# A scheduled graph-network kernel: a priority table for each batch by itself, and batch 14's mirrored products taken back to TensorE

## The chip, the cores and the metric

The kernel runs on 1 core of one Trainium2 chip. Its time is the device time of one execution in microseconds (us); the figure for the kernel before is the median of 9 executions, 2457.01 us (2454.72 to 2459.84). Beside it there is a profile of one execution, from which all durations below are read. The engines are named as the profile names them: PE (TensorE, the matrix products; PEld is its loading of weights), DVE (VectorE), ACT (ScalarE), POOL (GpSimd) and SP (SyncE, which issues DMAs here and computes nothing).

## The reference

Sixteen batches of 1024 nodes with 128 features pass through four graph layers. Each layer first normalises and clips its input, and its result is added to `x`. All is float32.

```python
h = jnp.maximum(_layernorm(x, axis=-1), 0.0)          # ahead of each layer
# layer 0: three products in a row
h = h @ W + b
nh = h / jnp.maximum(jnp.linalg.norm(h, axis=-1, keepdims=True), EPS)
cos = jnp.einsum('bij,bkj->bik', nh, nh)              # 1024 x 1024, symmetric
h = jnp.einsum('bpq,bqc->bpc', edge_weight * cos, h)  # relu after the first two
# layer 1
x_agg = jnp.einsum('bnf,bnm->bmf', x, adjacency)
y = jnp.maximum(((1.0 + eps) * x + x_agg) @ W1 + b1, 0.0) @ W2 + b2
# layer 2
attn = jax.nn.softmax(where(att_mat > 0, tanh(s1[:, :, None] + s2[:, None, :]), NEG_INF), axis=-1)
last_h = jnp.einsum('bij,bjf->bif', attn, h)
# layer 3
e = jnp.einsum('bil,bkl->bik', h @ A, h)
e = e + jnp.swapaxes(e, 1, 2)                         # 1024 x 1024, symmetric
att = jax.nn.softmax(where(adj > 0, e, 0), axis=1) * adj
h_prime = relu(att @ h); i, f, o = three gates, each sigmoid(concat([x, h_prime]) @ w + b)
out = o * tanh(sigmoid(i * h_prime + f * x))
```

Each batch so has four symmetric 1024 x 1024 products: three in layer 0 (called products 0, 1 and 2 here) and one in layer 3 (product 3). Beside them stand the adjacency times features of layers 0 to 3, six accumulations over 1024 nodes.

## The kernel before, in words

A batch's nodes lie in 8 blocks of 128. A 1024 x 1024 matrix is made in 8 rows `j`, each in two halves `s` of 128 x 512 (one bank of PSUM). For a symmetric product only the blocks on and above the diagonal are multiplied (`sq`, line 768). The blocks below are mirrored from those above: the copies kept in the tile `above` are transposed on PE into the same bank (line 778), and what fills `above` is an ACT copy (line 800). For most batches the 4 x 4 quarter of blocks in the lower left goes another way (`Square`, `by_dma`): DVE transposes the right halves of rows 0 to 3 in squares of 32 x 32 into `above` (line 790), SP sends them to HBM in two parts (`by_hbm`, line 810), and eight DMAs bring them back with the squares in their places into the tile `got` (line 821), from which DVE reads the left halves of rows 4 to 7. The function `far` (line 533) says for which batches this holds: before, batches 1 to 14.

In a row, DVE turns the product into the weights of the accumulation: in layer 0 by `ew` (line 967); in layer 3 by `e` (line 1185, two halves), the row's largest value `top` (line 1197), an exponential on ACT (line 1201) that also gives the row's sum, its reciprocal (line 1215), a multiplication by the adjacency (line 1210) and a scaling of `hs` on ACT (line 1219). In batch 14 POOL does that multiplication for the odd rows (line 1206). Layer 2 has a tanh and an exponential per row on ACT (lines 1109, 1113) and one masking on DVE (line 1117). PE then adds the row to the accumulators (lines 830 and 841). Each layer starts with a normalisation on DVE, POOL (`rstd`, line 570) and ACT (lines 678 to 734), and layer 3 ends with gates (`finish`): in batch 14 its five wide steps stand on POOL (lines 1289, 1290, 1314), in batch 15 on DVE in two halves (lines 1296, 1308).

No order is written by hand. The kernel records every operation with an engine, an assumed duration, its reads and its writes. The class `Plan` then lists them (`order`): it keeps a clock for each engine, takes the engine whose next operation could start first, and among the operations of that engine that could start within `WINDOW` it issues the one with the smallest rank. The rank is a batch's deadline, less the length of the work that hangs on the operation, less a lead:

```python
lead = self.leads.get(o.key + o.edge, self.leads.get(o.key, 0.0))
o.rank = (self.deadline(o.batch) - o.tail - lead, o.seq)
```

A key is layer, engine and tile, such as `3 DVE e3`. The lead comes from the table `LEADS`: one value per key for all batches, with values of their own (`o.edge`) for batches 0, 1, 14 and 15. The deadlines are `PERIOD` 59 apart, batch 15's stands `LAST` 22 behind batch 14's. At most `AHEAD` 2 batches are open beyond the oldest. `POOLS` gives the number of buffers of each pool, and `KINDS` for each kind of tile the pool, the most buffers that it may hold and the most that batches younger than the oldest may hold. The listed order is what each engine's queue executes; an engine waits at an instruction whose inputs aren't there, and everything behind it in that queue waits too. Each batch's loads (`adjT`, `adjL`, `x`) and the round trips of `above` are issued in SP's queue, the stores of the result and the parameters in ACT's.

Of the kernel before, what the change touches and what calls it, by code (L numbers as in the profile page):

```python
# [53 lines left out]
class Plan:  # L54
# [53 lines left out]
    def link(self):  # L108
# [23 lines left out]
        for o in reversed(self.ops):  # L132
            o.tail = o.us + max((s.tail + o.lat for s in o.succs), default=0.0)
            lead = self.leads.get(o.key + o.edge, self.leads.get(o.key, 0.0))
            o.rank = (self.deadline(o.batch) - o.tail - lead, o.seq)
# [87 lines left out]
def tile_adj_preln(  # L223
# [67 lines left out]
    FLAGS = set("CabcdkxhyzTu")  # L291
# [34 lines left out]
    for load_it in first:  # L326
# [11 lines left out]
    POOLS = {"adjT": 16, "adjL": 5, "x": 3, "big": 13, "above": 2, "got": 1, "bank": 8, "small": 25, "row": 6, "hbm": 3, "hrow": 2}  # L338
    KINDS = {
        "adjT": ("adjT", 16, 16), "adjL": ("adjL", 5, 5), "x": ("x", 3, 3), "w4": ("big", 12, 12),  # L340
        "chunk": ("big", 9, 7), "above": ("above", 2, 1), "got": ("got", 1, 1), "ps": ("bank", 8, 7),
        "acc": ("bank", 7, 4), "small": ("small", 12, 8), "row": ("row", 5, 4), "hbm": ("hbm", 3, 2),
        "hrow": ("hrow", 2, 1),
    }
    PERIOD, LAST, AHEAD, WINDOW = 59.0, 22.0, 2, 0.05

    LEADS = {
        "0 ACT hT": -65.5, "0 DVE hn": -25.5, "0 DVE mv": 7, "0 DVE nb": -71, "0 DVE st": -1.5, "0 PE ps": -69,
        "0 POOL rstd": -10.5, "00 ACT above": 72.5, "00 ACT hT": -105.5, "00 ACT sq": 8, "00 DMA by": 83.5,
        "00 DMA got": 6.5, "00 DVE above": -17.5, "00 DVE ew": 50, "00 DVE h": -94, "00 DVE ss": -97,  # L350
        "00 PE acc0": -327, "00 PE ps": -234, "00 PE psP": 32, "00 PE sq": 124.5, "00 POOL rn": -50,
        "01 ACT above": 9, "01 ACT hT": 49, "01 ACT hTn": 145, "01 ACT sq": 358.5, "01 DMA by": -11.5,
        "01 DMA got": -20.5, "01 DVE above": 74.5, "01 DVE ew": 115, "01 DVE h": -7.5, "01 DVE ss": -16,
        "01 PE acc0": -170.5, "01 PE ps": -23, "01 PE sq": -68.5, "01 POOL rn": -16.5, "02 ACT above": -16,
        "02 ACT hTn": -101.5, "02 ACT sq": -56, "02 DMA by": -62, "02 DVE above": 3.5, "02 DVE ew": -96,
        "02 DVE ss": -6.5, "02 DVE x": -69, "02 PE acc0": -50.5, "02 PE ps": -19.5, "02 PE psP": 8.5,
        "02 PE sq": 284, "02 POOL rn": -16.5, "1 ACT g": 56.5, "1 ACT hn": 29, "1 ACT y1": 0.5,
        "1 DMA adjL": -175, "1 DVE adjL": 21, "1 DVE hn": -246.5, "1 DVE mv": 2, "1 DVE nb": -35.5,
        "1 DVE st": -772.5, "1 PE acc1": 3.5, "1 PE py": -151, "1 PE py2": -6.5, "1 POOL rstd": 31,
        "2 ACT e2": -115, "2 ACT h": 530.5, "2 ACT hfl": -66.5, "2 ACT hn": 7.5, "2 ACT hnT": 1.5,  # L360
        "2 ACT s1": -39.5, "2 DVE alone": -27.5, "2 DVE e2": 92, "2 DVE h": -0.5, "2 DVE hn": -12.5,
        "2 DVE hrow": -2.5, "2 DVE mv": 2.5, "2 DVE nb": 109, "2 DVE rden": -25.5, "2 DVE st": 10,
        "2 DVE x": 28.5, "2 PE acc2": 94.5, "2 PE p1": -12, "2 PE pf": -67.5, "2 PE ps": 9.5,
        "2 PE psP": -355.5, "2 POOL rstd": 5, "3 ACT above": -40, "3 ACT e3": 4, "3 ACT gT": -23.5,
        "3 ACT h3T": 51.5, "3 ACT hn": -43.5, "3 ACT hnT": 48.5, "3 ACT hp": 93.5, "3 ACT hpT": -21,
        "3 ACT z": -228, "3 DMA by": 11.5, "3 DMA z": -83.5, "3 DVE e3": -370, "3 DVE gate": 6.5,
        "3 DVE h": -79.5, "3 DVE hn": 217, "3 DVE mv": 16, "3 DVE nb": 220.5, "3 DVE st": -260.5,
        "3 DVE sum": -13, "3 DVE top": 42.5, "3 DVE z": -826, "3 PE acc3": -141.5, "3 PE pg": -19,
        "3 PE ps": 68.5, "3 PE psN": 171, "3 PE psP": 474.5, "3 POOL rstd": -22, "3 POOL z": -14,
        "T ACT adjT": 4, "T DMA adjT": -179, "T DVE adjT": -519.5, "x DMA x": -11.5, "0 ACT hT <0": -52.5,  # L370
        "0 ACT hT <1": 32, "0 ACT hT >0": -61, "0 ACT hT >1": 40.5, "0 ACT hn <0": -66, "0 ACT hn <1": -4.5,
        "0 ACT hn >0": 18.5, "0 ACT hn >1": -72, "0 DVE hn <0": -42.5, "0 DVE hn <1": 23.5,
        "0 DVE hn >0": -47.5, "0 DVE hn >1": -107, "0 DVE mv <0": 24, "0 DVE mv <1": 0, "0 DVE mv >0": 39,
        "0 DVE mv >1": 23, "0 DVE nb <0": -33.5, "0 DVE nb <1": -75, "0 DVE nb >0": 2, "0 DVE nb >1": -115.5,
        "0 DVE st <0": 3, "0 DVE st <1": 1, "0 DVE st >0": 23.5, "0 DVE st >1": -43, "0 PE ps <0": 63,
        "0 PE ps <1": -50.5, "0 PE ps >0": 49, "0 PE ps >1": 55.5, "0 POOL rstd <0": -5.5, "0 POOL rstd <1": 1,
        "0 POOL rstd >0": -83.5, "0 POOL rstd >1": -11, "00 ACT above <0": 25.5, "00 ACT above <1": 103.5,
        "00 ACT above >0": 141, "00 ACT above >1": 21, "00 ACT hT <0": -102.5, "00 ACT hT <1": -46,
        "00 ACT hT >0": 19.5, "00 ACT hT >1": 49, "00 ACT hTn <0": 0.5, "00 ACT hTn <1": 96.5,
        "00 ACT hTn >0": -73, "00 ACT hTn >1": -16.5, "00 ACT params <0": 1.5, "00 ACT sq <0": -4,  # L380
        "00 ACT sq <1": 120, "00 ACT sq >0": -83, "00 ACT sq >1": -5, "00 DMA by <1": -12, "00 DMA by >1": -1.5,
        "00 DMA got <1": 1.5, "00 DMA got >1": -3.5, "00 DMA params <0": -41.5, "00 DVE above <1": -252.5,
        "00 DVE above >1": -194, "00 DVE ew <0": 333, "00 DVE ew <1": 33.5, "00 DVE ew >0": -6.5,
        "00 DVE ew >1": -152, "00 DVE h <0": 0.5, "00 DVE h <1": 0.5, "00 DVE h >0": 4.5, "00 DVE h >1": 14,
        "00 DVE params <0": 391.5, "00 DVE ss <0": 4, "00 DVE ss <1": 8.5, "00 DVE ss >0": -1,
        "00 DVE ss >1": -7, "00 PE acc0 <0": -108, "00 PE acc0 <1": -172.5, "00 PE acc0 >0": -98,
        "00 PE acc0 >1": -312, "00 PE params <0": 79, "00 PE ps <0": 2.5, "00 PE ps <1": -117,
        "00 PE ps >0": -52.5, "00 PE ps >1": -107, "00 PE psP <0": 85, "00 PE psP <1": 42.5, "00 PE psP >0": 31,
        "00 PE psP >1": -14.5, "00 PE sq <0": 90, "00 PE sq <1": 185, "00 PE sq >0": 72, "00 PE sq >1": 250.5,
        "00 POOL rn <0": -42.5, "00 POOL rn <1": -48, "00 POOL rn >0": -46, "00 POOL rn >1": -25.5,  # L390
        "01 ACT above <0": 12.5, "01 ACT above <1": 11.5, "01 ACT above >0": -6.5, "01 ACT above >1": -1,
        "01 ACT hT <0": 52.5, "01 ACT hT <1": 93.5, "01 ACT hT >0": 38, "01 ACT hT >1": 24,
        "01 ACT hTn <0": 40.5, "01 ACT hTn <1": 110.5, "01 ACT hTn >0": 117.5, "01 ACT hTn >1": 107.5,
# [1049 lines left out]
```

## Time and profile before

| | |
|---|---|
| median of 9 executions | 2457.01 us (2454.72 to 2459.84) |
| the profiled execution: own time, span of its profile | 2459.84 us, 2458.0 us |
| PE busy | 2393.3 us, 97% of the span |
| DVE busy | 2118.3 us, 86% |
| ACT busy | 1270.8 us, 52% |
| POOL busy | 230.5 us, 9% |
| PE's share of the chain that ended last | 89% |
| moved by DMA | 271.75 MB, mean 111 GB/s |

A matmul in float32 leaves two records in the trace, a transpose on PE one. Their ends are modelled, and the records of one engine overlap; what a matmul costs PE in a dense stretch is the distance from its start to the next start. "Busy" merges such records, so that a short wait between two matmuls can be hidden under a record's end. PEclk is the clock that TensorE was granted, as a share of full speed.

### The profile page before, as it was taken

What the parts mean: (1) busy time and instruction counts of PE and PEld (TensorE: products, weight loads), DVE (VectorE), ACT (ScalarE), POOL (GpSimd) and SP (SyncE); (2) the same over time, 40 slices, a digit from 0 to 9 for tenths busy, and PEclk for the clock granted to TensorE, in tenths of its full rate; (3) what the DMA queues carried; (4) which work ended last, traced back from release to release, by engine and by line L of the source; (5) the groups of instructions that cost most, each with busy time, mean ns of one, the idle gap of its engine ahead of it and who ended that gap; (6) DMA issues with size and microseconds to landing.
All of it is one profiled execution on the core that took longest, in us unless ns stands there. A gap on an engine that the chain in (4) does not pass through costs nothing.

```text
span 2458.0 us, 34785 instructions
## 1 busy us (share of the span) xinstructions
PE 2393.3 (97%) x11882; PEld 1587.5 (65%) x11882; DVE 2118.3 (86%) x5280; ACT 1270.8 (52%) x2388; POOL 230.5 (9%) x141
## 2 busy tenths in 40 slices
PE   6999999999999999999999999999999999999995
PEld 3568576775757667576765766667576765665763
DVE  5758989899899989889898999989889899886586
ACT  3426564645545464463645545474464646543564
POOL 1001010100101001010101101001010110101012
PEclk9999999999999999999999999999999999999998
DMA  8831929658393774929657393874929568582010
GB/s 126 131 103 35 171 53 157 135 85 156 78 171 95 128 147 78 179 52 164 128 91 153 80 170 91 134 141 86 173 59 162 123 94 166 82 97 69 27 35 17
DMA packets 1171074, 271.75 MB, mean 111 GB/s; under 512 B 1005264, under 2 KB 1154512, under 8 KB 1170896
## 3 DMA queue, kind: packets, MB, share of 16 engines
q1 hardware_dynamic: 1149968, 260.12, 60.4%
q10 hardware_dynamic: 20928, 9.40, 1.4%
q8 instruction: 94, 1.54, 0.3%
q14 instruction: 84, 0.69, 0.1%
HBM read 202.33 MB, written 67.11 MB: 110 GB/s over the span
## 4 chain that ended last, share of the span: by engine, by line
PE 89%; DVE 4%; DMA 3%; ACT 2%; SPq 1%; issue 1%; POOL 0%; POOLq 0%; ACTq 0%; DVEq 0%
PE acc L830 34%; PE sq L768 18%; PE acc L841 17%; PE psP L608 5%; PE sq L778 4%; PE py L618 2%; PE py L1029 2%; PE ps_hTn L577 2%; PE pg L618 1%; PE ps_hnT L577 1%; PE psN L608 1%; DVE e L1185 1%; DMA by_hbm<-above 1%; DVE ew L967 1%; DMA got<-by_hbm 1%; PE ps_hT L577 1%
## 5 line engine op out<-in xcount | busy, mean ns | idle before, releaser
L830 PE MATMUL acc<-ew,h 128*128 128x512 f32 x1024 | 482.5, 597 | 6.6 <-DVE ew L967 6.5
L967 DVE SCALAR_TENSOR_TENSOR ew<-sq,rn,adjT 128x512 f32<-128x512 f32 x600 | 422.1, 738 | 36.7 <-PE sq L768 13.9
L768 PE MATMUL sq<-hTn 128*128 128x512 f32 (+3 forms) x1152 | 430.0, 488 | 0.4 <-ACT hTn L630 0.3
L800 ACT COPY above<-sq 128x256 f32<-128x256 f32 (+3 forms) x416 | 159.0, 386 | 471.2 <-PE sq L768 255.4
L768 PEld LDWEIGHTS sq<-hTn 128*128 128x128 f32 x1152 | 198.7, 191 | 147.1 <-issue 101.7
L830 PEld LDWEIGHTS acc<-ew,h 128*128 128x128 f32 x1024 | 180.0, 191 | 168.9 <-issue 130.1
L841 PEld LDWEIGHTS acc<-h,ew 128*128 128x128 f32 x2048 | 244.3, 192 | 31.8 <-issue 17.0
L830 PE MATMUL acc<-e,hs 128*128 128x512 f32 x512 | 247.3, 607 | 11.6 <-DVE e L1210 6.2
L841 PE MATMUL acc<-h,ew 128*128 128x128 f32 x2048 | 254.2, 275 | 0.1
L830 PE MATMUL acc<-adjL,hn 128*128 128x512 f32 x512 | 236.8, 598 | 4.8 <-ACT hn L734 4.8
L1201 ACT ACTIVATE e<-e,top 128x1024 f32<-128x1024 f32 x128 | 147.1, 1149 | 179.5 <-DVE top L1197 171.6
L841 PEld LDWEIGHTS acc<-h,e 128*128 128x128 f32 x2048 | 232.6, 192 | 11.1 <-issue 4.5
L841 PE MATMUL acc<-h,e 128*128 128x129 f32 x2048 | 234.3, 275 | 1.7 <-DVE e L1117 1.0
L570 POOL TENSOR_TENSOR rstd<-ve,mhalf 128x8 f32<-128x8 f32 x64 | 105.1, 1642 | 1250.2 <-DVE ve L689 1140.9
L898 ACT ACTIVATE adjT<-adjT 128x1024 f32<-128x1024 f32 x128 | 135.1, 1056 | 150.2 <-DVE adjT L895 104.0
L778 PEld LDWEIGHTS sq<-ident,above 128*128 128x128 f32 x896 | 118.9, 142 | 122.8 <-issue 92.4
L790 DVE STREAM_TRANSPOSE above<-sq 128x512 f32<-128x512 f32 x224 | 157.6, 707 | 35.1 <-PE sq L768 34.3
L895 DVE STREAM_TRANSPOSE adjT<-adjT 128x1024 f32<-128x1024 f32 x128 | 154.4, 1224 | 23.1 <-DMA adjT<-in_adj_dram 21.6
L778 PE MATMUL sq<-ident,above 128*128 128x128 f32 x896 | 165.9, 274 | 4.4 <-ACT above L800 4.4
L1117 DVE SCALAR_TENSOR_TENSOR e<-adjT,e 128x512 f32<-128x512 f32 x256 | 158.4, 679 | 7.5 <-ACT e L1113 7.4
L1210 DVE TENSOR_TENSOR e<-e,adjT 128x512 f32<-128x512 f32 x248 | 163.4, 679 | 0.0
L713 ACT ACTIVATE hn<-x,nb,rstd 128x128 f32<-128x128 f32 x256 | 105.4, 483 | 102.4 <-DVE nb L697 92.7
(130 smaller groups left out, 3507.2 us busy)
## 6 DMA issues: line engine op xcount, KB each, us to landing
adjT<-in_adj_dram SPq DMA_DIRECT2D x512, 128.0 KB, 4.3
adjL<-in_adj_dram SPq DMA_DIRECT2D x128, 512.0 KB, 5.0
by_hbm<-above SPq DMA_DIRECT2D x112, 512.0 KB, 4.2
got<-by_hbm SPq DMA_DIRECT2D x448, 128.0 KB, 3.9
x<-in_x_dram SPq DMA_DIRECT2D x15, 512.0 KB, 5.0
out_dram<-z ACTq DMA_DIRECT2D x15, 512.0 KB, 5.7
x<-in_x_dram SPq DMA_DIRECT2D x2, 256.0 KB, 4.6
out_dram<-z ACTq DMA_DIRECT2D x2, 256.0 KB, 2.7
```

What stands on the lines that cost most here:

```text
L608: nc.tensor.matmul(dst.t[:, (c - lo) * n : (c - lo + 1) * n], cols(srcT.t, c), w, start=True, stop=True)
L768: lambda: nc.tensor.matmul(dst.t[:, (first - lo) * P :], cols(leftT.t, j), span(rightT.t, first, hi), start=True, stop=True),
L778: nc.tensor.transpose(cols(dst.t, r), cols(above.t, p), ident)
L790: lambda: nc.vector.transpose(span(above.t, p, p + 4), read.t),
L800: lambda: nc.scalar.copy(span(above.t, p, p + hi - first), read.t[:, (first - lo) * P :]),
L830: lambda s=s, lo=lo, hi=hi: nc.tensor.matmul(acc[s].t, cols(h.t, at, w), span(ew.t, lo, hi), start=(j == 0), stop=(j == NB - 1)),
L841: nc.tensor.matmul(a.t[:, (c - lo) * n : (c - lo + 1) * n], cols(ew.t, c), h.t[:, at * w : at * w + n], start=(j == 0 and c == lo), stop=( ...
L895: dve(V(N), [t], [t], lambda t=t: nc.vector.transpose(t.t, t.t), True)
L967: lambda view=view, ew=ew, rn=rn, j=j, lo=lo, hi=hi: nc.vector.scalar_tensor_tensor(by_block(span(ew.t, lo, hi), D, 4), view(), rn.t[:, j ...
L1117: lambda e=e, j=j, lo=lo, hi=hi: nc.vector.scalar_tensor_tensor(span(e.t, lo, hi), span(aT[j].t, lo, hi), 0.0, span(e.t, lo, hi), op0=ALU. ...
L1201: lambda e=e, top=top, tot=tot: nc.scalar.activation(e.t[:, 0:N], e.t[:, 0:N], AF.Exp, bias=top.t, accum_out=tot.t),
L1210: lambda e=e, j=j, lo=lo, hi=hi: nc.vector.tensor_mul(span(e.t, lo, hi), span(e.t, lo, hi), span(aT[j].t, lo, hi)),
```

## The change

- The lead is looked up for each key and each batch: `LEADS[key]` is now a tuple of 16 values. The values are others throughout, and the special keys for the first and last two batches are gone. Where the old table's special values covered 4 of 16 batches, now the order of every batch may differ from its neighbour's.
- The flag `u` is gone, so that `far` holds for batches 1 to 13. Batch 14's four symmetric products mirror all their lower blocks on PE, as batches 0 and 15 do already: no round trip through HBM, and ACT copies where DVE transposed.
- `PERIOD` 59 becomes 60 and `LAST` 22 becomes 52: batch 15's deadline stands 52 behind batch 14's.
- `small` has 29 buffers in place of 25, and the shares in `KINDS` are others: `ps` may hold 5 of the 8 banks of PSUM (before 8, of which 7 for younger batches), `acc` 8 (before 7), `chunk` 11 (9), `w4` 12 of which 8 for younger batches (12), `small` 7 (12), `row` 3 (5).

```diff
-            lead = self.leads.get(o.key + o.edge, self.leads.get(o.key, 0.0))
+            lead = self.leads[o.key][o.batch] if o.key in self.leads else 0.0
...
-    FLAGS = set("CabcdkxhyzTu")
+    FLAGS = set("CabcdkxhyzT")
...
-    POOLS = {"adjT": 16, "adjL": 5, "x": 3, "big": 13, "above": 2, "got": 1, "bank": 8, "small": 25, "row": 6, "hbm": 3, "hrow": 2}
+    POOLS = {"adjT": 16, "adjL": 5, "x": 3, "big": 13, "above": 2, "got": 1, "bank": 8, "small": 29, "row": 6, "hbm": 3, "hrow": 2}
     KINDS = {
-        "adjT": ("adjT", 16, 16), "adjL": ("adjL", 5, 5), "x": ("x", 3, 3), "w4": ("big", 12, 12),
-        "chunk": ("big", 9, 7), "above": ("above", 2, 1), "got": ("got", 1, 1), "ps": ("bank", 8, 7),
-        "acc": ("bank", 7, 4), "small": ("small", 12, 8), "row": ("row", 5, 4), "hbm": ("hbm", 3, 2),
+        "adjT": ("adjT", 16, 16), "adjL": ("adjL", 5, 5), "x": ("x", 3, 3), "w4": ("big", 12, 8),
+        "chunk": ("big", 11, 4), "above": ("above", 2, 1), "got": ("got", 1, 1), "ps": ("bank", 5, 5),
+        "acc": ("bank", 8, 6), "small": ("small", 7, 6), "row": ("row", 3, 3), "hbm": ("hbm", 3, 2),
         "hrow": ("hrow", 2, 1),
     }
-    PERIOD, LAST, AHEAD, WINDOW = 59.0, 22.0, 2, 0.05
+    PERIOD, LAST, AHEAD, WINDOW = 60.0, 52.0, 2, 0.05
     LEADS = {
-        "0 ACT hT": -65.5, "0 DVE hn": -25.5, "0 DVE mv": 7, "0 DVE nb": -71, "0 DVE st": -1.5, "0 PE ps": -69,
...
-        "3 DVE e3": -370, "3 DVE e3 <0": -117.5, "3 DVE e3 <1": -399.5, "3 DVE e3 >0": -355, "3 DVE e3 >1": -521,
...
+        "3 DVE e3": (39.5, -336, -321, -314.5, -286.5, -296, -271, -307.5, -382, -319, -343.5, -253, -427, -402, -335, -152.5),
...
     }
...
-        o.edge = f" <{now[0]}" if now[0] < 2 else f" >{B - 1 - now[0]}" if now[0] > B - 3 else ""
```

(The five old values of `3 DVE e3` stand at different places of the old table and are brought together here.) The function that the flag reaches is unchanged:

```python
def far(b, product):
    return (b > 0 or "v" in FLAGS and product > 0) and b < (B - 1 if "u" in FLAGS else B - 2)
```

In the listed order of the changed program, against that of the program before, PE has 64 transposes more of line 778, DVE 16 transposes of 128 x 512 fewer (line 790), ACT 16 copies of 128 x 512 more (line 800), and SP 8 sends of line 810 and 32 loads of line 821 fewer. All other instructions are the same in number; most stand in another order from the first batch on.

## The prediction

> **What bounds the kernel now.** I read the page's busy shares, its forty slices, the busy time by stretches, the waits, and the timelines of PE and DVE at the end.
>
> ```profile
> PE 2393.3 (97%) x11882; PEld 1587.5 (65%) x11882; DVE 2118.3 (86%) x5280; ACT 1270.8 (52%) x2388; POOL 230.5 (9%) x141
> ...
> PE   6999999999999999999999999999999999999995
> ```
>
> ```profile
> 0.00:61.45 61.45, 38.62 (x148) 23.63 (x149) 36.33 (x100) 23.61 (x47) 8.92 (x11) 0.94 0.82 126
> ...
> 1045.00:1198.00 153.00, 153.00 (x775) 102.39 (x774) 139.66 (x356) 82.77 (x157) 13.33 (x8) 1.00 0.63 118
> ...
> 2397.00:2458.00 61.00, 34.99 (x115) 18.95 (x114) 37.04 (x82) 25.94 (x53) 14.87 (x7) 0.80 0.06 18
> ```
>
> In a stretch of the middle PE is busy for 153.00 of 153.00 us; only the first and the last slices have room. Busy time can hide short waits, so I price PE by distances from start to start:
>
> ```profile
> 1000.52 5.31 PE L830 MATMUL acc<-adjL,hn 128*128 128x512 f32 x12
> 1005.67 0.27 PE L778 MATMUL sq<-ident,above 128*128 128x128 f32 x1
> ...
> 2166.96 1.39 PE L830 MATMUL acc<-e,hs 128*128 128x512 f32 x2 [1.91 <-ACT e L1201]
> 2168.66 7.45 PE L830 MATMUL acc<-e,hs 128*128 128x512 f32 x14 [0.31 <-DVE e L1210]
> ...
> 2273.30 1.15 PE L778 MATMUL sq<-ident,above 128*128 128x128 f32 x9
> 2274.28 0.60 PE L577 MATMUL ps_hnT<-ident,hn 128*128 128x128 f32 x4
> ...
> 2276.37 12.67 PE L841 MATMUL acc<-h,ew 128*128 128x128 f32 x112
> 2288.88 1.95 PE L608 MATMUL psP<-w2e,hnT 128*128 128x130 f32 x16
> ...
> 2296.35 13.60 PE L830 MATMUL acc<-adjL,hn 128*128 128x512 f32 x26 [4.42 <-ACT hn L734]
> ...
> 2317.13 3.73 PE L1029 MATMUL py<-w,y 128*128 128x128 f32 x32
> 2320.70 6.86 PE L841 MATMUL acc<-h,e 128*128 128x129 f32 x60
> ...
> 2437.49 2.08 PE L608 MATMUL psN<-eye,hpT 128*128 128x131 f32 x16
> ```
>
> A record of 512 columns takes 5.15/12 = 0.429 us, a transpose 0.98/9 = 0.109, a record of 128 to 131 columns 12.51/112 = 0.112 (384 and 256 columns 0.322 and 0.215 in proportion). By the groups of shapes there are 3008, 1924, 6432, 256 and 256 of them: 1290 + 210 + 720 + 82 + 55 = about 2358 us of work at full rate. Some 100 of the span's 2458 us are left: 12 before the first matmul, 18 up to 61 us, 10 from there to 2089, 7 to 2289, 7 to 2321 (4.42 of it the wait at 2296.35), 45 from 2321 to the end, of which 18.6 lie behind PE's last matmul (2439.4). So nothing can be won in the middle; the change wins or loses in the last 170 us and by the work that it gives to PE.
>
> **The change, part by part.** The program's order, priced with these distances, has 2357.8 us of PE work before and 2364.8 after.
>
> *The flag.* 64 transposes more in batch 14: 64 x 0.109 = +7.0 us, on the path, since PE is full. DVE loses 16 transposes at 0.64 us from start to start, ACT gains 16 copies at 0.49, SP's queue loses 40 DMAs; ahead of 2289 us all of that lies beside PE, I cost it at nothing, and were PE's cover gone DVE's 10 us would be a gain. Behind 2289 it is in the walk below.
>
> *Deadlines, pools and shares* issue nothing; they act through the order alone.
>
> *The start.* SP's first 16 loads stand in the same order and the waits there end with `adjT` loads (DVE sits 5.01 and 5.36 us for them): 0, between -2 and +2.
>
> *The middle (61 to 2089).* All 13 batches are reordered. What I can read from the order is how much PE work stands between the last product of a row and its first accumulation, which is the time that DVE and ACT have. In layer 3 the least of a batch (2 to 11) was 9.1 us and is 10.0 to 12.1; in layer 0 the median of the rows was 2.5 to 3.8 and is 1.8 to 4.7. The round trip of `got` had at least 13 us of PE work in the three products of layer 0 and has 13 (42 and 40 in layer 3). Before, these distances sufficed without waits, so 0; the bounds are -5 (half of the 10 us that are there) and +18 (twelve batches with a wait of 1.5 us, the size of the wait at 2166.96).
>
> *2089 to 2289.* The wait at 2166.96 is batch 13's layer 3: there the least distance was 5.1 us, now it is 16.2. The wait and the half rate behind it (2 records in 1.70 us, 0.85 each) go: 7 us idle become 3, -4 (bounds 0 and -6).
>
> *2289 to 2321.* Batch 15's `x`, statistics, `rstd` and `hn` take 7.4 us behind the last `acc` of layer 0 (2288.9 to 2296.3). Before, 3.4 us of PE work stood there (line 608, 1072, 1098); now 8.1 us of batch 14's layer 2 do. Late next are the additions to the sixth and seventh `adjL` block, which stand on DVE behind batch 14's `hn`: I walk that to 2 us. 7 become 2.5: -4.5 (bounds 0 and -7).
>
> *From batch 15's last `py2` on.* Before, it ends at 2320.9, and 137.1 us follow with 92.5 us of PE work: layer 2 of both batches, then both layers 3 interleaved, batch 14's last. Now 80.1 us of work follow: batch 14's layer 3 runs beside batch 15's layer 2, then batch 15's layer 3 runs alone. I walk it with DVE's rows:
>
> ```profile
> 2392.63 1.29 DVE L1185 SCALAR_TENSOR_TENSOR e<-adjT,sq 128x512 f32<-128x512 f32 x2 [0.18 <-ACT above L800]
> 2393.95 1.22 DVE L1197 TENSOR_REDUCE top<-e 128x1 f32<-128x1024 f32 x1
> ...
> 2408.51 1.27 DVE L1210 TENSOR_TENSOR e<-e,adjT 128x512 f32<-128x512 f32 x2
> ```
>
> Start to start, a half row of line 1185, 1210 or 1117 costs 0.60, a `top` 1.13, a reciprocal 0.07. First the overlap: `py2` to `hrow` takes 11 us (before: 2320.9 to 2331.5). Then DVE has 14's rows and 15's maskings, 32.8 us, ACT 30 us of exponentials and copies beside it; I add 4 for DVE at exponentials and at POOL's four multiplications of 2.35. Layer 2's end and the next normalisation (lines 1130 to 1138, 652, 678, 687, 570, 706) take 9.5. Sum 57.3 with 48.5 of PE work: 9 idle. Then alone: from the transposes of `hn` to the first row 10 (11.5 for batch 14 at 2354.9, where `nb` came after `hn`); rows 16 x 0.60 + 8 x 1.13 + 8 x 0.07 + 16 x 0.60 = 28.8; 3 at their start, because batch 14's two `z` activations (2.2) stand ahead of the first exponentials on ACT; last accumulation, `hpT` and `psN` 5; the finish on DVE in halves 8.5, and the store 4.2 (2453.8 to 2458.0). Sum 59.5. Together 116.8 in place of 137.1: -20.3 (bounds -28, if DVE never waits and the prologue is 7; -10, if each of the two phases gets 5 us of waits more). `py2` itself ends 19.4 us of PE work later (2364.8 - 80.1 against 2357.8 - 92.5), the 7.0 among them.
>
> *The sum:* +19.4 - 4 - 4.5 - 20.3 = -9.4 us of the profiled span. That execution took 2459.84, 2.8 over the median; I take the difference over: 2457.0 - 9.4 = **2447.6 us**.
>
> [...] The row: a wait of 1.91 us already brought half rate (above), and in the last 61 us the granted clock is 0.80. So I took the prologue and the last accumulation at partly half rate. [...]
>
> **The rivals.**
> - *The overlap saves nothing.* The walk holds no waits that I did not look for. For it: before, ten waits of 0.5 to 2.9 us stand in the last 100 us. Against: they add up to some 13 us, and the walk is padded with 7. With 5 to 10 us more the time is 2452 to 2462, no change.
> - *The lone layer is paced by a cold PE.* Between its first row and its last, PE has 10.9 of products and 13.8 of accumulations, 24.7 us; at half rate 49, in place of DVE's 31.8: +17, 2465, slower. It decides from 29 us of half rate on, at a loss of half of it (14.3 us lead from -9.4 to +4.9). For it: the 0.80. Against: at full rate PE would be busy for three quarters of these rows.
> - *New waits in the middle.* With 1.5 us in each of twelve batches +18: 2466. For it: PE has no slack there, a wait is paid in full. Against: the distances above.
> - *Better still:* the unpadded walk, 2437 or less.
>
> The change can't do nothing: the order differs on each engine.
>
> **How the numbers follow.** No change is within 0.2%, 4.9 us, about what a measurement of this kernel can tell. Forecast (2437 to 2452) 0.63, better still 0.04, the saving eaten 0.17, cold PE 0.07, waits in the middle 0.09. Faster 0.67, same 0.17, slower 0.16. The range reaches from 2436 to 2462: 0.04 below, 0.16 above.
>
> **What would show it.** Right: line 778 with 960 records; PE busy 153 of 153 us in the middle; no wait of batch 13's layer 3 and none of 4 us at layer 1 of batch 15; about 13 us from the last matmul to the end in place of 18.6; 117 us from batch 15's last `py2` to the end. Wrong: waits of PE for `ew` or `e` spread over the middle, or a granted clock under 0.8 in the last 60 us.

## The result and the profile after

The changed kernel takes 2446.73 us, the median of 9 executions (2442.65 to 2450.59); the kernel before, run beside it, 2456.84 (29 executions, 2452.45 to 2461.88). The ratio is 0.9959, with a 95% interval of 0.9951 to 0.9967: 10.1 us less, or 0.41%. The prediction said 2447.6 and 9.4 us less. The profiled execution took 2447.29, its span is 2445.5.

The number was met, the reasons only in part. The page of the changed kernel, busy shares and PE's row of the forty slices, and below them the two lines of the chain of waits:

```profile
PE 2390.7 (98%) x11946; PEld 1587.3 (65%) x11946; DVE 2117.4 (87%) x5264; ACT 1283.2 (52%) x2404; POOL 232.0 (9%) x141
...
PE   6999999999999999999999999999999999999997
...
PE 81%; DVE 9%; DMA 5%; ACT 2%; SPq 2%; issue 1%; ACTq 0%; POOL 0%; DVEq 0%; POOLq 0%
PE acc L832 30%; PE acc L843 17%; PE sq L770 16%; PE psP L610 5%; PE sq L780 3%; DVE ew L969 3%; DMA got<-by_hbm 2%; DMA by_hbm<-above 2%; PE py L620 2%; PE py L1031 2%; PE ps_hTn L579 1%; PE pg L620 1%; DVE e L1187 1%; SPq L823 1%; DVE top L1199 1%
```

PE is busier (98% for 97%), and yet its share of the chain has fallen from 89% to 81%: DVE's `ew` and the round trip of `above` to `got` are on the path now. (Lines of the changed kernel stand two higher than those of before.) The stretches that answer to those shown of before, with time, busy us of each engine, granted clock of PE, DMA share and GB/s:

```profile
0.00:61.45 61.45, 41.09 (x161) 24.61 (x162) 38.15 (x105) 28.05 (x56) 8.92 (x11) 0.94 0.88 134
1045.00:1198.00 153.00, 152.88 (x762) 100.96 (x761) 141.48 (x357) 83.00 (x160) 13.32 (x8) 1.00 0.64 117
2384.50:2445.50 61.00, 43.61 (x167) 23.81 (x165) 43.54 (x113) 32.10 (x64) 11.86 (x6) 0.93 0.06 18
```

The stretch of the middle looks as full as before (152.88 for 153.00). That is a warning about a single stretch: the middle lost 14 us, in waits that stand elsewhere, and the same view of all of it, 61.45 to 2060 us, shows PE busy for 1985.45 us of 1998.55 where it was 1996.37. In the last 61 us PE is busy for 43.6 us in place of 35.0, at a clock of 0.93 in place of 0.80.

PE's timeline at the places of which the prediction spoke:

```profile
2307.43 8.21 PE L843 MATMUL acc<-h,e 128*128 128x129 f32 x72
2315.47 11.32 PE L832 MATMUL acc<-adjL,hn 128*128 128x512 f32 x26
...
2333.75 3.73 PE L1031 MATMUL py<-w,y 128*128 128x128 f32 x32
...
2422.45 10.55 PE L832 MATMUL acc<-e,hs 128*128 128x512 f32 x20 [1.92 <-DVE e L1212]
2432.84 2.05 PE L610 MATMUL psN<-eye,hpT 128*128 128x131 f32 x16
```

The first `acc` of batch 15's layer 1 (2315.47) has no wait before it any more, where 4.42 us stood; 8 us of batch 14's layer 2 lie in between (2307.43). Batch 15's last `py2` ends at 2337.3, and the program 108.2 us later, where it had been 137.3. From PE's last matmul to the end it is 10.8 us, where it had been 18.6. Line 780 (778 before) has 960 records, 64 more.

Priced as in the prediction (a stretch's length less its records times 0.429, 0.322, 0.215, 0.112 or 0.109 us), the time in which PE does no work at full rate is this. The third column starts where batch 14 begins to set the order; `py2` is batch 15's last.

| us | PE work | 0 to 61.45 | 61.45 to 2060 | 2060 to `py2` | behind `py2` | span |
|---|---|---|---|---|---|---|
| before | 2358.9 | 29.8 | 9.5 | 14.9 | 44.9 | 2458.0 |
| after | 2365.9 | 26.9 | 24.4 | 0.1 | 28.1 | 2445.5 |
| difference | +7.0 | -2.9 | +14.9 | -14.8 | -16.8 | -12.5 |

So the change gained 32 us in the last 385 us and 3 at the start, and gave back 7 for the transposes and 15 in the middle. (The two profiled executions differ by 12.5, the medians by 10.1: that of before was 2.8 above its median.)

The waits of PE in the middle, from 61 to 2060 us, in total, count and longest; before:

```profile
PE acc L830 <- DVE ew L967: 0.4, 2, 0.3
PE acc L830 <- ACT hn L734: 0.4, 1, 0.4
```

and after:

```profile
PE acc L832 <- DVE ew L969: 7.5, 10, 2.4
PE pf L1074 <- DVE hrow L1067: 3.0, 2, 1.6
```

Set against the program's order, nearly all of the `ew` waits are one place: the rows 4 to 7 of product 0, the first that read `got`, in batches 4 to 7 and 9 to 11. They hold 8.5 us of the time without work at full rate there (under 0.1 before). The two waits for `hrow` stand among the same rows of batches 12 and 13; with these two batches it is 12.0 us (0.5 before). Batch 9 has the longest wait. In SP's queue, DVE, POOL and PE of the changed kernel, around it:

```profile
1306.88 15.52 SPq L889 DMA_DIRECT2D adjT<-in_adj_dram  x16
1322.50 0.88 SPq L812 DMA_DIRECT2D by_hbm<-above  x1
...
1327.60 2.33 SPq L823 DMA_DIRECT2D got<-by_hbm  x4
```

```profile
1319.45 0.70 DVE L792 STREAM_TRANSPOSE above<-sq 128x512 f32<-128x512 f32 x1
...
1333.67 1.42 DVE L969 SCALAR_TENSOR_TENSOR ew<-got,rn,adjT 128x512 f32<-128x512 f32 x2 [1.41 <-DMA got<-by_hbm]
...
1335.09 3.06 DVE L969 SCALAR_TENSOR_TENSOR ew<-got,rn,adjT 128x512 f32<-128x512 f32 x2
...
1335.75 2.40 DVE L969 SCALAR_TENSOR_TENSOR ew<-got,rn,adjT 128x512 f32<-128x512 f32 x1
...
1338.07 0.74 DVE L969 SCALAR_TENSOR_TENSOR ew<-sq,rn,adjT 128x512 f32<-128x512 f32 x1
```

```profile
1335.32 2.28 POOL L1316 TENSOR_TENSOR z<-hn,gate 128x1024 f32<-128x1024 f32 x1 [4.38 <-DVE gate L1305]
```

```profile
1334.72 1.02 PE L832 MATMUL acc<-ew,h 128*128 128x512 f32 x2
1335.58 0.81 PE L770 MATMUL sq<-hTn 128*128 128x384 f32 x2
1336.22 0.27 PE L780 MATMUL sq<-ident,above 128*128 128x128 f32 x1
1338.86 1.13 PE L832 MATMUL acc<-ew,h 128*128 128x512 f32 x2 [2.37 <-DVE ew L969]
```

The squares are ready at 1320.15; their send waits in SP's queue behind 16 issues of `adjT` until 1322.50; the loads into `got` are issued at 1327.60, and DVE gets them at 1333.67, after 1.41 us of waiting. Then the four halves of rows 4 to 7 that read `got` come first in DVE's queue, and the right half of row 4 only at 1338.07. PE reaches the second accumulation of row 4 with 2.37 us to wait.

The row of 3.06 us holds two halves, and the second of them (the row of 1335.75) takes 2.40 us where such a half takes 0.74. It begins while POOL multiplies `hn` by a gate of an earlier batch into `z` (1335.32 to 1337.60), and it ends 0.55 us behind that product. Six halves of the changed kernel are held up in this way, in batches 6 and 8 to 12, for 2.13 to 2.40 us each; each ends 0.55 us behind POOL's product, and the 150 other halves of `ew` that read `got` take 0.75 at most. In batch 13 DVE's `alone` ahead of `hrow` is held up (1.50 us for 0.17). The four halves that read `sq` beside that product keep their 0.74 to 0.75. Before, the product was done 2 to 4 us ahead of the first of these halves in each of batches 4 to 13, and none of the 168 is held up; for the batch that is shown it ended at 1328.63 and the halves began at 1331.56:

```profile
1326.72 1.91 POOL L1314 TENSOR_TENSOR z<-hn,gate 128x1024 f32<-128x1024 f32 x1 [35.10 <-issue]
```

```profile
1331.56 2.74 DVE L967 SCALAR_TENSOR_TENSOR ew<-got,rn,adjT 128x512 f32<-128x512 f32 x4 [0.82 <-DMA got<-by_hbm]
```

So two things meet in the middle: `got` is late for the first accumulation of row 4 in batches 4, 5 and 7 (1.4 us of waits), and POOL's product holds DVE up in front of an accumulation of row 4 or of `hrow` in batches 6 and 9 to 13 (7.9 us of waits). If every held operation had taken its usual time, some 6.9 us of these 7.9 would not be there; that is an estimate from these rows, since no run here moved POOL's product alone.

The round trip itself is hardly longer than before. From the last transpose to DVE's first read of `got`, in batches 4 to 13, it takes 12.5 us on average (12.4 before). What differs is the order. Before, these batches have all the same one: 16.0 us of PE work from row 3's last product to the first accumulation of row 4, 19.1 to the second. After, each batch has its own: 14.2 to 17.6, and 18.2 to 19.1; and in batches 9 to 11 the small product `pf`, which waits for DVE's `hrow`, stands right behind that accumulation.

### The profile page after: what moved, and what is told of

Read it like the earlier page. It is cut to its first block, busy times and chain, and to the rows that moved or that the text cites. A ratio compares the mean times of both kernels' runs of the same rounds, so it can differ in the third digit from the quotient of the medians.

```text
span 2445.5 us, 34793 instructions
## 1 busy us (share of the span) xinstructions
PE 2390.7 (98%) x11946; PEld 1587.3 (65%) x11946; DVE 2117.4 (87%) x5264; ACT 1283.2 (52%) x2404; POOL 232.0 (9%) x141
## 3 DMA queue, kind: packets, MB, share of 16 engines
q8 instruction: 94, 1.54, 0.3%
## 4 chain that ended last, share of the span: by engine, by line
PE 81%; DVE 9%; DMA 5%; ACT 2%; SPq 2%; issue 1%; ACTq 0%; POOL 0%; DVEq 0%; POOLq 0%
PE acc L832 30%; PE acc L843 17%; PE sq L770 16%; PE psP L610 5%; PE sq L780 3%; DVE ew L969 3%; DMA got<-by_hbm 2%; DMA by_hbm<-above 2%; PE py L620 2%; PE py L1031 2%; PE ps_hTn L579 1%; PE pg L620 1%; DVE e L1187 1%; SPq L823 1%; DVE top L1199 1%
## 5 line engine op out<-in xcount | busy, mean ns | idle before, releaser
L832 PE MATMUL acc<-ew,h 128*128 128x512 f32 x1024 | 482.6, 596 | 13.5 <-DVE ew L969 13.4
L969 DVE SCALAR_TENSOR_TENSOR ew<-sq,rn,adjT 128x512 f32<-128x512 f32 x612 | 432.4, 738 | 57.8 <-ACT above L802 27.6
L802 ACT COPY above<-sq 128x256 f32<-128x256 f32 (+3 forms) x432 | 167.6, 394 | 399.1 <-PE sq L780 203.5
L843 PEld LDWEIGHTS acc<-h,e 128*128 128x128 f32 x2048 | 233.3, 192 | 14.9 <-issue 5.7
L780 PEld LDWEIGHTS sq<-ident,above 128*128 128x128 f32 x960 | 126.2, 142 | 123.6 <-issue 88.8
L780 PE MATMUL sq<-ident,above 128*128 128x128 f32 x960 | 175.2, 274 | 1.1 <-ACT above L802 0.8
L792 DVE STREAM_TRANSPOSE above<-sq 128x512 f32<-128x512 f32 x208 | 146.5, 707 | 21.3 <-PE sq L770 20.4
```

The costliest lines, as they stand in the source:

```text
L780: nc.tensor.transpose(cols(dst.t, r), cols(above.t, p), ident)
L792: lambda: nc.vector.transpose(span(above.t, p, p + 4), read.t),
L802: lambda: nc.scalar.copy(span(above.t, p, p + hi - first), read.t[:, (first - lo) * P :]),
L832: lambda s=s, lo=lo, hi=hi: nc.tensor.matmul(acc[s].t, cols(h.t, at, w), span(ew.t, lo, hi), start=(j == 0), stop=(j == NB - 1)),
L843: nc.tensor.matmul(a.t[:, (c - lo) * n : (c - lo + 1) * n], cols(ew.t, c), h.t[:, at * w : at * w + n], start=(j == 0 and c == lo), stop=( ...
L969: lambda view=view, ew=ew, rn=rn, j=j, lo=lo, hi=hi: nc.vector.scalar_tensor_tensor(by_block(span(ew.t, lo, hi), D, 4), view(), rn.t[:, j ...
```

## The experiments

In e2, e3, e5, e6 and e9 the planner ranks by two tables or deadlines, one up to a switch and the other from there on, with the shares that belong to each; so the middle of one kernel is joined to the end of the other. Their line numbers are up to 148 higher. The flag `u` is out in all of the kernels below, so their operations are those of the changed kernel, but for what e4, e7, e8 and e9 add or move. The "lone layer" is batch 15's layer 3, which stands alone behind all other work.

| | median, us | ratio to before, 95% interval |
|---|---|---|
| changed kernel | 2446.73 | 0.9959 [0.9951, 0.9967] |
| e1 flag alone | 2459.15 | 1.0005 [0.9996, 1.0013] |
| e2 changed middle, old end | 2467.50 | 1.0038 [1.0024, 1.0052] |
| e3 old middle, changed end | 2434.59 | 0.9906 [0.9892, 0.9920] |
| e4 send from ACT's queue | 2458.94 | 1.0005 [0.9996, 1.0013] |
| e5 = e3 with the old deadline | 2452.41 | 0.9978 [0.9968, 0.9988] |
| e6 = e1 with the new deadline at the end | 2453.19 | 0.9980 [0.9969, 0.9991] |
| e7 `top` twice in the lone layer | 2457.42 | 0.9998 [0.9989, 1.0007] |
| e8 transposes twice in the lone layer | 2446.78 | 0.9952 [0.9939, 0.9964] |
| e9 = e3 with three rows on POOL | 2431.90 | 0.9900 [0.9885, 0.9915] |
| e10 right half of row 4 first | 2444.73 | 0.9949 [0.9937, 0.9962] |

And where PE did no work at full rate, from one profile of each:

| us | 0 to 61.45 | 61.45 to 2060 | 2060 to `py2` | behind `py2` | `py2` to the end |
|---|---|---|---|---|---|
| e1 | 29.0 | 11.3 | 10.9 | 40.8 | 139.2 |
| e2 | 27.7 | 24.3 | 10.0 | 39.1 | 137.6 |
| e3 | 30.3 | 8.3 | 0.3 | 28.2 | 108.2 |
| e4 | 26.9 | 34.9 | 0.1 | 27.9 | 108.1 |
| e5 | 29.4 | 9.2 | 1.0 | 46.4 | 128.7 |
| e6 | 29.0 | 10.9 | 21.1 | 27.7 | 121.9 |
| e7 | 26.9 | 23.2 | 0.1 | 37.8 | 118.0 |
| e8 | 27.7 | 22.5 | 0.1 | 24.9 | 108.1 |
| e9 | 29.4 | 8.3 | 0.2 | 25.8 | 105.8 |
| e10 | 28.1 | 21.2 | -0.1 | 28.2 | 108.2 |

### e1: the flag alone

```diff
-    FLAGS = set("CabcdkxhyzTu")
+    FLAGS = set("CabcdkxhyzT")
```

> The kernel before with nothing changed but the flag u, so that batch 14 mirrors its quarter on PE: 64 transposes more, 16 transposes of DVE fewer, 40 DMAs fewer, the old table, old deadlines and shares. By the prediction's step the 64 transposes of 0.109 us are paid in full: 2456.8 + 7.0 = 2463.8, ratio 1.0028. The rival: DVE loses 16 x 0.64 = 10 us in batch 14, and the last 140 us of the old order are set by DVE; then part or all of the 7 comes back there, and the time is between 2455 and 2459.

The work of PE grows by the 7.0 us, but the time by 1.2 (0.05%, between -1.0 and +3.2): the rival holds. Beside the profile of before, 4.0 us come back between 2060 and `py2` and 4.1 behind it, where DVE's 16 transposes and the round trips of batch 14 are gone. So with the old table the 64 transposes are nearly free; the new table with the flag was not run.

### e2 and e3: the two middles and the two ends exchanged

In both the planner got

```diff
             o.rank = (self.deadline(o.batch) - o.tail - lead, o.seq)
+            early = self.early[o.key][o.batch] if o.key in self.early else 0.0
+            o.rank_early = (min(o.batch * self.due[0], (self.batches - 2) * self.due[0] + self.due[1]) - o.tail - early, o.seq)
...
-                        pool, most, share = self.kinds[k]
+                        pool, most, share = (self.early_kinds if oldest < self.switch else self.kinds)[k]
...
-                key=lambda f: f[1].rank,
+                key=lambda f: f[1].rank_early if oldest < self.switch else f[1].rank,
```

with the changed table early and `switch` 13 in e2, the old table early and `switch` 12 in e3.

> Spliced in the planner: as long as the oldest open batch is below 13 the operations are ranked with the changed table, deadlines and shares, from there on with the old ones; the flag u is out, so the operations are those of the changed kernel. It is to be read against the run with the flag alone, which has the same operations and the same end of the order. If the 24 us in which PE doesn't work between 61 and 2089 us of the changed kernel (10 before) belong to its order, this run is 8 to 14 us slower than the flag alone. If they are an accident of the one profiled execution, it is within 2 us of the flag alone.

> The splice the other way round: old table, deadlines and shares while the oldest open batch is below 12, the changed ones from there on; flag u out. If the changed kernel wins in its last 350 us and loses in the middle, this one has both good parts: idle in the middle 10 to 12 us in place of 24, from batch 15's last py2 to the end 108 us as in the changed kernel, time 2432 to 2438, ratio about 0.991. If the good end depends on how the batches stand when it begins, or if the waits of the middle come with batch 14 on PE and not with the table, the time is 2444 or more, as in the changed kernel.

e2 is 8.3 us slower than e1, which has the same operations and the same end. Its middle is idle for 24.3 us as in the changed kernel, and the same waits are there, with six `got` halves held up by POOL's product again (1.70 to 2.40 us). PE's waits from 61 to 2060 us in e2:

```profile
PE acc L978 <- DVE ew L1115: 6.6, 10, 2.5
PE pf L1220 <- DVE hrow L1213: 1.6, 2, 0.8
```

and in e3, the longest that there is, beside a second of the same length:

```profile
PE sq L924 <- ACT above L946: 0.3, 1, 0.3
```

e3 takes 2434.59 us, 24.6 less than e1 and 12.1 less than the changed kernel; its end is that of the changed kernel to a tenth (28.2 idle, 108.2 us from `py2` on). In e3 no half that reads `got` takes over 0.77 us. So the waits of the middle belong to the new table and shares (the two were not parted) and not to one execution, nor to batch 14's flag, and the good end doesn't depend on that middle. The two parts of the change can be had apart, and their sum is near: e1 + 8.3 - 24.6 = 2442.9, against 2446.73.

### e4: the second send of product 0 from ACT's queue

```diff
-                lambda: nc.sync.dma_start(
+                lambda: (nc.scalar if lo == 2 and self.k.endswith("_0") else nc.sync).dma_start(
```

> The changed kernel; only the second send of product 0 (by_hbm, rows 2 and 3) is issued from ACT's queue in place of SP's, where in batches 4 to 12 it stands behind the 16 to 32 issues of the adjT loads and goes out 0.3 to 3 us after its data is there. If SP's queue makes the first row that reads got late, the waits of PE for ew_4 of product 0 (7.6 us in batches 4 to 11) shrink to 2 or less and the time goes to 2439 to 2442. If the flight of the DMAs itself sets the round trip, the waits and the time stay (2446 +- 1.5). If ACT is held up by the issue and the wait in its queue, new waits of PE for ACT appear and it is slower than the changed kernel.

It is 12.2 us slower than the changed kernel, as the third case had it, but not for the reason given there: PE's waits for ACT in the middle grew by 0.6 us only (1.3 to 1.9). The send went out hardly earlier, because in ACT's queue it stands behind other work: on average over batches 4 to 13 it left 1.25 us after the last transpose, in place of 1.54. And the rest of the round trip grew, so that DVE got `got` 13.5 us after the last transpose in place of 12.5. The middle has 10.5 us more of idle PE, of which 7.6 stand at rows 4 to 7 of product 0. The trip grew in six of the ten batches (4, 5, 6, 10, 12 and 13, by 0.9 to 3.2 us) and shrank in the other four (by 0.2 to 0.8), and the idle time at these rows grew in the same six and shrank in the same four. The experiment failed as a cure for SP's queue, and why the later part of the trip grew was not settled. That an earlier send would win was not shown. What the ten batches do show is that in this order a longer round trip is paid where it falls.

### e5 and e6: deadline and leads of the end

e5 is e3 with

```diff
-    PERIOD, LAST, AHEAD, WINDOW = 60.0, 52.0, 2, 0.05
+    PERIOD, LAST, AHEAD, WINDOW = 59.0, 22.0, 2, 0.05
```

and e6 is e1 with `switch` 12, behind which the old table and the old shares go on with 60.0 and 52.0.

> As the run with the old middle and the changed end (2434.6 us), but the deadlines of the end are the old ones too: batch 15's stands 22 behind batch 14's in place of 52. Table and shares of the end stay the changed ones. If the end is won because batch 15's layer 3 comes alone, behind batch 14's, and the deadline brings that, both layers 3 are interleaved again, the idle time of PE behind batch 15's last py2 goes back from 28 us to 41 to 45, and the time is 2447 to 2452. If the leads of batches 14 and 15 carry the end by themselves, it stays at 2434 to 2438.

> As the run with the flag alone (2459.2 us: old table, old shares, flag u out), but from the time at which batch 12 is the oldest on batch 15's deadline stands 52 behind batch 14's and PERIOD is 60. If the deadline is the cause of the shorter end, the part behind batch 15's last py2, less the PE work in it, goes from 41 us to 28, and the time to 2445 to 2449. If it needs the new leads as well, the idle time ahead of py2 (11 us there) grows by what is won behind it or the end keeps its 41 us, and the time is 2456 or more.

e5: without the new deadline the end is lost, 46.4 us of idle in place of 28.2, and 17.8 us of time. PE's waits there:

```profile
2331.98 2.10 PE L723 MATMUL ps_hnT<-ident,hn 128*128 128x128 f32 x8 [7.64 <-DVE hn L852]
...
2380.21 2.08 PE L976 MATMUL acc<-e,hs 128*128 128x512 f32 x2 [6.71 <-DVE e L1356]
```

e6: the deadline alone brings the short end (27.7 us idle), but ahead of it the idle time grows from 10.9 to 21.1, and the time falls by 6.0 us only. (Its profiled execution was 3.2 us over its median.) The accumulations of the two layers 3 show the same: in e5 batch 15's begin at 2407.4, ahead of the end of batch 14's (2418.7); in e6 they follow each other (2415.0 and 2415.9), as they do in the changed kernel, with more room (2389.6 and 2410.7). The wait ahead of batch 15's layer 1, which the changed kernel has lost, is there as in the kernel before:

```profile
2307.64 4.63 PE L978 MATMUL acc<-adjL,hn 128*128 128x512 f32 x5 [4.42 <-ACT hn L882]
```

Neither theory holds by itself. The deadline is what shortens the part behind `py2`; the new leads, with the new shares that come with them, are what keeps the part ahead of it free of waits (21.1 to 0.3 us, e6 against e3).

### e7 and e8: what paces batch 15's lone layer

```diff
-                lambda e=e, top=top: nc.vector.tensor_reduce(top.t, e.t[:, 0:N], axis=AX.X, op=ALU.max, negate=True),
+                lambda e=e, top=top: [
+                    nc.vector.tensor_reduce(top.t, e.t[:, 0:N], axis=AX.X, op=ALU.max, negate=True)
+                    for _ in range(2 if b == B - 1 else 1)
+                ],
```

```diff
-                    for r, p in enumerate(at):
-                        nc.tensor.transpose(cols(dst.t, r), cols(above.t, p), ident)
+                    for r, p in enumerate(at * (2 if self.k == "15_3" else 1)):
+                        nc.tensor.transpose(cols(dst.t, r % len(at)), cols(above.t, p), ident)
```

> The changed kernel; in batch 15's layer 3 each row's top is computed twice (8 reductions of 1.13 us more on DVE, the second writes the same values, the listed order is the same). If DVE paces that lone layer, the time grows by 8 to 10 us, to 2455 to 2457. If PE paces it (24.7 us of matmuls and transposes between first row and last, in 29.8 us), DVE has room and it grows by 4 or less.

> The changed kernel; in batch 15's layer 3 each mirrored block is transposed twice on PE (112 transposes of 0.109 us more, 12.2 us, the second writes the same values). If DVE paces the lone layer the time grows by 0 to 5 us (the added work lies in PE's waits), if PE does, by 10 to 12.

The 8 reductions of 1.13 us, 9.0 us, lengthen the part behind `py2` by 9.8 us and the time by 10.7: they are paid in full. The expectation of e8 has a wrong count: 112 blocks are mirrored in the four products of a batch, in the one product of layer 3 it is 28, so 3.06 us were added and not 12.2. They cost nothing that can be seen (+0.05 us in the medians, with intervals of some 3 us either way; the end is 108.1 us long, its idle time 3.2 less). DVE paces the lone layer. One stretch of the changed kernel's profile says the same, from the first `e` to the last:

```profile
2400.44:2430.20 29.76, 23.57 (x75) 11.56 (x74) 29.41 (x48) 18.26 (x35) 6.60 (x4) 0.94 0.06 18
```

DVE (the third busy time) works for 29.41 of 29.76 us, PE for 23.57.

### e9: three rows on POOL

e3 with

```diff
-            if ("5" in FLAGS or "z" in FLAGS and (b == B - 2 if "T" in FLAGS else b >= B - 2)) and j % 2:
+            if (b == B - 2 and j % 2 or b == B - 1 and j in (0, 1, 3)):
```

(and the condition of the loop below it changed in the same way).

> As the run with the old middle and the changed end (2434.6 us), but in batch 15's layer 3 POOL multiplies rows 0, 1 and 3 by the adjacency, as it does for the odd rows of batch 14: DVE loses 6 halves of 0.60 us, 3.6 us. If DVE paces the lone layer, the time falls by 2 to 3.6, to 2431 to 2432.5. If a multiplication of 2.35 us on POOL takes longer than the row has, the accumulations wait for it and the time stays at 2434.6 or grows.

2431.90 us, 2.7 less than e3 by the medians (by the ratios 1.5, and their intervals overlap); the end is 2.4 us shorter, of the 3.6 that DVE is spared. That is about the same price from the other side, and the fastest kernel here: 0.9900 of before, 14.8 us under the changed kernel.

### e10: the right half of row 4 first

The changed kernel with its listed order changed by hand in product 0 of batches 4 to 11:

```diff
     ordered = plan.order()
+    for b in range(4, 12):
+        ew = [o for o in ordered if o.key == "00 DVE ew" and o.batch == b]
+        of = lambda o, j: any(t.name == f"ew_{b}_0_{j}" for t in o.bufs)
+        left = lambda o: any(t.kind == "got" for t in o.bufs)
+        right4 = next(o for o in ew if of(o, 4) and not left(o))
+        for o in reversed([o for o in ew if left(o) and (of(o, 5) or of(o, 6) or of(o, 7))]):
+            k = ordered.index(right4)
+            if ordered.index(o) < k < min(ordered.index(s) for s in o.succs | o.after):
+                ordered.remove(o)
+                ordered.insert(ordered.index(right4) + 1, o)
```

> The changed kernel with one step of the listed order moved by hand: in product 0 of batches 4 to 11 DVE computes the right half of ew_4 (from sq, no round trip) ahead of the left halves of rows 5 to 7 (from got), two or three of 0.7 us each; in the changed kernel it stands behind all of them. PE's order is the same. If the waits of PE for the second accumulation of row 4 (0.9 us in batch 6, 2.5 in 9, 1.1 in 10, 0.9 in 11) are that queue's doing, they go and the time is 2441 to 2443. If the late landing of got is all that counts, PE waits as much at row 5 and the time stays at 2446 +- 1.5.

Between the two theories: 2.0 us less in time, where the intervals overlap, and 3.2 in the idle time of the middle. In batches 6 and 9 to 11 the waits at the second accumulation of row 4 are gone. In 9 to 11 PE waits in their place for `hrow` a matmul later, because the moved halves now stand in front of it on DVE:

```profile
1335.06 0.75 DVE L969 SCALAR_TENSOR_TENSOR ew<-sq,rn,adjT 128x512 f32<-128x512 f32 x1 [1.11 <-ACT above L802]
...
1335.72 2.15 DVE L969 SCALAR_TENSOR_TENSOR ew<-got,rn,adjT 128x512 f32<-128x512 f32 x3
...
1337.79 0.27 DVE L1067 TENSOR_SCALAR hrow<-hsum 128x128 f32<-128x128 f32 x1
...
1338.21 0.46 PE L1074 MATMUL pf<-w2f,hrow 128*128 128x128 f32 x2 [1.03 <-DVE hrow L1067]
```

So the order of DVE's queue decides where PE waits, but the work that stands there has to be done behind a late `got` in any case. How much of the 3.2 us is the order's own is open: in batches 9 and 10 POOL's product now runs while DVE has almost no half of `got` to compute, and no half is held up there by more than 0.1 us, while in batches 6, 8, 11 and 12 one still is (1.56 to 2.40 us). Which of the many moved operations of these batches would have to go back, one by one, was not tried.

## Why the prediction was right, and where it was not

The forecast of 2447.6 lies 0.9 us from the median, and its case, faster by more than 0.2%, came true. That it lies so near is luck: the middle lost 14.0 us that the sum did not have, and the other parts gained 17 us more than it had. In time without work at full rate, each term of the sum against the profile after:

| term | predicted | measured |
|---|---|---|
| PE's work: 64 transposes | +7.0 | +7.0 |
| start | 0 (-2 to +2) | -2.9 |
| middle, 61 to 2089 | 0 (-5 to +18) | +14.0 |
| 2089 to batch 15's last `py2` | -8.5 (-13 to 0) | -13.9 |
| behind `py2` | -7.9 | -16.8 |
| sum | -9.4 | -12.5 |

**The flag.** The +7.0 was worked out rightly as work, and put wrongly "on the path, since PE is full": by e1 the flag costs 1.2 us, since 8 us of waits at the end go with batch 14's transposes on DVE and its round trips. The prediction had weighed that relief only ahead of 2289, and costed it at nothing.

**The middle** is the step that failed. It rested on distances in PE's order: the "round trip of `got` had at least 13 us of PE work in the three products of layer 0 and has 13", and "before, these distances sufficed without waits, so 0". Three things are wrong with it. The least of three products says nothing of the one that is tight: before, product 2 had 13 us and waited for nothing, product 0 had 16.0 and needed 15.5 (the transposes end 2.3 us after row 3's product, the trip takes 12.4, and 0.8 lies between the start of DVE's read and PE's). In it the second send stands behind the `adjT` loads in SP's queue, a queue that was not walked. And only the first accumulation of row 4 was looked at, not the second, whose half stands behind four others on DVE. And nothing was asked of what runs beside these halves: POOL's product into `z` holds one of them up by 1.4 to 1.7 us in six batches, and 7.9 of the 9.3 us of waits at row 4 and at `hrow` come behind such a held operation. That a distance sufficed before said nothing of how much was left: it was some tenths of a microsecond. Of the rivals, "new waits in the middle" came true, at 14 us of the 18 it named, though for the largest part in nine batches and not in twelve. The sign that was named for it, waits of PE for `ew` spread over the middle, is the one that showed; the full stretch from 1045 to 1198 us, named as a sign of the opposite, lies where hardly any of them stand. Three readings in the working are a little off and decided nothing: the wait at 2166.96 is 1.91 us and not 1.5 (the bound would be +23 with it), the least distance of `got` in layer 3 (batches 2 to 11) is 36.6 us after and not 40, and the PE work ahead of 2296.35 is 3.0 us and not 3.4.

**The start** was put at 0, at most 2 either way. The runs with the changed table's start are idle there for 26.9 to 28.1 us, those with the old one for 29.0 to 30.3; some 2 us so belong to the order or the shares. Before, PE waits there for an ACT copy into `above` (4.1 us); in the changed kernel that wait is gone, and 1.4 us more stand ahead of batch 0's `hT`.

**2089 to `py2`.** Both waits went, batch 13's in layer 3 and the 4.42 us ahead of batch 15's layer 1, as predicted. Mis-sized were the remainders: 3 and 2 to 2.5 us had been left for what is late next, and 0.2 is there in all. e6 says that the new leads, with the new shares, did it.

**Behind `py2`.** The mechanism was right (e5: the deadline brings batch 15's layer 3 to stand alone; e7, e8: DVE paces it), and the length was 108.2 in place of 116.8, below its lower bound (137.1 - 28 = 109.1). The terms: the overlap 55.0 us for 57.3; the lone layer 53.1 for 59.5, of which the prologue 8.1 for 10 (2392.36 to 2400.44), the rows 29.8 for 28.8 + 3, the last accumulation to `psN` 4.5 for 5, finish and store 10.8 for 12.7. Most of the padding was unneeded; the walk over DVE's durations, 28.8 us for the rows against 29.8, was the sound part. The rivals that ate the saving did not come.

**The clock.** The prediction took part of the lone layer at half rate. By the granted clock there was one such piece ahead of the last matmul, of 3.41 us; before, there were 17.1 us of them behind `py2`. The first row is that of before, the second that of after:

```profile
2416.81:2427.05 10.24, 8.92 (x20) 4.98 (x20) 8.17 (x14) 5.06 (x10) 2.77 (x2) 0.50 0.00 0
```

```profile
2423.01:2426.42 3.41, 3.41 (x6) 1.25 (x4) 3.41 (x6) 0.87 (x3) 0.00 (x0) 0.50 0.00 0
```

The piece at half rate came behind a wait of 1.92 us (ahead of 2422.45), as the one of before that the prediction went by came behind 1.91 us (ahead of 2166.96); the rest of the layer up to the last matmul ran at full rate.

## What to carry to other kernels

When an engine is full, read its slack where it is least, and for each product by itself: walk every queue that the trip passes (here SP's loads and DVE's other halves) and what the other engines run beside it (here POOL's product, beside which halves of 0.74 us on DVE took up to 2.40), because an order that shows no waits may sit within tenths of a microsecond of them. A reordering of everything is a sum of separate parts with both signs; joining the old middle to the new end (e3) took 12 us more off than the whole change had, and showed which part was which. Where one engine paces a stretch, changing its work a little in both directions (e7 up, e9 down) gives its price, and doubling that of its neighbour (e8) shows what is free.

## What the runs showed of the hardware that was not expected

**POOL's product and DVE.** In the changed kernel six halves of `ew` that read `got` and `adjT` began while POOL's product into `z` (1.91 to 2.35 us) ran. They were not slowed in proportion: each ended 0.55 us behind the product, after 2.13 to 2.40 us in place of 0.74. The four halves beside it that read `sq`, which this kernel keeps in PSUM, took 0.74 to 0.75 us. Beside POOL's short `rstd` (1.64 us, on 128 x 8) no half that reads `got` was held up: six of before and two of the changed kernel began while it ran and took 0.75 us at most. The held halves are there in other runs with the new middle too (e2: six of 1.70 to 2.40 us; e10: four of 1.56 to 2.40), and in two with the old one there is none (before: 0.76 us at most; e3: 0.77).

**The granted clock.** In the profiles of before and after, each stretch at one granted clock, from one change to the next, lasted a whole number of 3.41 us (1 to 695 of them). Cut on that grid from 2050 us to the last matmul, the two profiles have 216 windows at full rate and 9 at half rate that another window follows. Of those at full rate, the five in which PE worked for 16 to 37% of the time were each followed by half rate; of three with 39 to 40%, one was; of the 208 others, with 47% or more, none. Of those at half rate, three with PE at work for 25, 70 and 75% were followed by another; one with 73% was not, nor were five with 86% or more. Two neighbours from the changed kernel, both at full rate:

```profile
2371.78:2375.20 3.42, 1.61 (x14) 1.42 (x13) 3.42 (x5) 3.42 (x6) 1.72 (x1) 1.00 0.00 0
2419.59:2423.01 3.42, 1.50 (x4) 0.41 (x3) 3.42 (x7) 2.02 (x5) 0.00 (x0) 1.00 0.00 0
```

The first has a wait of 1.80 us in it and 39% of work (by distances from start to start), and the next one ran at full rate too; the second has one of 1.92 and 33%, and the window behind it ran at half. It is a correlation over these two profiles; no run here was made to set the share.
